# Half of a depthwise convolution on TensorE, with merged weights, while VectorE makes the other half

## The chip, the cores and the metric

One NeuronCore of a Trainium2 chip runs the whole program. It has five engines with instruction streams of their own: TensorE (PE), VectorE (DVE), ScalarE (ACT), GpSimd (POOL) and SyncE (SP), which issues the DMAs here. The metric is the time of one execution on the device in microseconds; of several executions the median is given.

## The reference, cut to what matters

The input `x` is [4, 64, 64, 96]: four images. Two state-space layers (L0, L1) are followed by two layers of attention and feed-forward. Each state-space layer first normalises over groups of three channels and then does this (E = 192 inner channels):

```python
xz = jnp.einsum('bhwc,ec->bhwe', x, in_proj_w)
xx, z = jnp.split(xz, 2, axis=-1)
xc = conv_general_dilated(xx in NCHW, conv_w, (1, 1), [(1, 1), (1, 1)], feature_group_count=E) + conv_b
xc = silu(xc)
# four directions k of the image: row-wise, column-wise, and both reversed
x_dbl = einsum('bkdl,kcd->bkcl', xs, x_proj_weight)   # step sizes, B and C
delta = softplus(einsum('bkrl,kdr->bkdl', dts, dt_projs_weight) + bias)
h = exp(delta * A) * h + delta * B * u                # scan over 4096 positions
y = sum over directions of (C . h) + u * D; layer norm; y * silu(z); out_proj
```

The convolution is depthwise, 3 by 3, with a border of zeros: each of the 192 channels is a sum of nine shifted copies of its own plane, each times one number. The projection before it is linear and acts on channels alone. So projection and convolution together can also be written as nine matrices of 96 by 96, one for each tap: the matrix of tap t is the projection's weight times the tap's weight of each output channel.

## The kernel before, in words

**Stages.** The images are worked on in two pairs for each of the two state-space layers: four phases. `Scans.run` does for each phase first `prepare` (with `finish` of the phase before woven into it), then `scan_phase`. After the fourth scan comes its `finish` alone, then `token_layers`. All four scans have an order written out by hand. Everything else is emitted by Python generators, and a scheduler then decides the order in which each engine's instructions stand; that order is fixed when the program runs, and an engine never passes an instruction that waits. The order spoken of below is that of the built program.

**Preparation.** `prepare` takes the statistics of both images (`bn_stats`, L192), and then handles image 0 and image 1 of the pair. `convolve` does one image. Its 192 channels are two halves h of 96 (96 partitions each). For each half it loads the image in eight pieces of 512 positions (`rawi`, L252, two buffers), projects each on TensorE (L258), writes the result on ScalarE into a padded plane `xp` of 66 by 66 (L261), and then makes eight chunks of 512 outputs: ScalarE does tap 0 (L275), VectorE adds the other eight taps one instruction each (L277), ScalarE applies SiLU (L280). After a half's convolution it copies the result in another layout to `xu` (two buffers, L285) and stores it with eight DMAs to `ud` (L291), for the `D` term in `finish`. All of this is float32. `xp` and the rest of `convolve` live in a pool "conv" with one buffer, and image 1's pool can take the memory only when image 0's last `ud` store has landed.

`steps` makes, for one image, one chunk and one axis, the projections L300 (both halves are contracted, so both must be done) and L317, softplus, `du` and the three-part bfloat16 `delta`, and stores them. There are 32 such steps in a phase: 16 of image 0, into which image 1's `convolve` is woven (two `next(other)` a step), then 16 of image 1.

**Pace of finish.** Each `yield` of `prepare` adds `ph.beside` to an account; each whole unit in it lets `finish` go on by one `yield`. `finish` takes the phase's scan output in four quarters: permutation matmuls L603 and additions L612 for two halves, ScalarE copies L619, layer norm on VectorE (L642 to L657), gate L669 and L672, transposes L683, output projection L694. The first phase has no `finish` beside it.

Of the kernel before, what the change touches and what calls it, by code (L numbers as in the profile page):

```python
# [70 lines left out]
def view(t, off, *dims):  # L71

    return bass.AP(t.tensor, t.offset + off, [t.ap[0]] + [list(d) for d in dims])
# [57 lines left out]
class Scans:  # L131
# [19 lines left out]
    def prepare(self, ph):  # L151

        nc, cst, a, pre = self.nc, self.cst, self.a, ph.pre
        ph.gs = self.keep.tile([C, 2, 2], F32, name="gs", bufs=3)
        ph.delta = [
            self.dram.tile([G, NP16, E, TC], BF16, name="delta", bufs=2 * NC) for _ in range(NC)
        ]


        ph.du = [  # L160
            self.dram.tile([2, G, E + PITCH, TC], F32, name="du", bufs=2 * NC) for _ in range(NC)
        ]
        ph.bc = [self.dram.tile([NS // 2, G, 4, TC], F32, name="bc", bufs=2 * NC) for _ in range(NC)]
        ph.ud = self.dram.tile([C, 2, HW, 2, 64], F32, name="ud")
        ph.y = self.dram.tile([64, G, 2, 2, NEB, 16 * EB], F32, name="y")
        x = ph.x_in[ph.pair]

        with self.tc.tile_pool(name="prep", bufs=1) as wp, self.tc.tile_pool(
            name="steps", bufs=2
        ) as sp:  # L170

            def load(name, shape, at=0):
                t = wp.tile([at + shape[0]] + shape[1:], F32, name=name)
                nc.sync.dma_start(t[at:], a[pre + name])
                return t

            xp = load("x_proj", [C, 2, 2, XD2])
            dt_w = load("dt_w", [XD2 - 2 * NS, 2, E], at=2 * NS)
            conv_b = load("conv_b", [C, 2])
            ds = load("Ds", [C, 2, K])  # L180
            dsum = wp.tile([C, 2], F32, name="dsum")
            nc.vector.tensor_reduce(dsum, ds, mybir.AxisListType.X, ALU.add)
            yield


            st = wp.tile([C, 2, 8, 6], F32, name="st")
            with self.tc.tile_pool(name="stats", bufs=2) as rp:
                for hl in range(8):
                    raw = rp.tile([C, 8, 2, 64], F32, name="raw")
                    nc.sync.dma_start(raw, x[:, hl * 8 : hl * 8 + 8])  # L190
                    for i in range(2):
                        nc.vector.bn_stats(st[:, i, hl], raw[:, :, i])  # L192
                    yield
            for i in range(2):
                mv = wp.tile([C, 2], F32, name="mv")
                nc.vector.bn_aggr(mv, st[:, i].rearrange("p c s -> p (c s)"))
                ps = self.bank()
                nc.tensor.matmul(ps[:C, :1], cst.group, mv[:, 0:1], start=True, stop=True)
                gs = ph.gs[:, i]
                nc.vector.tensor_copy(gs[:, 0:1], ps[:C, :1])  # L200
                d = wp.tile([C, 1], F32, name="d")
                nc.vector.tensor_tensor(d, mv[:, 0:1], gs[:, 0:1], ALU.subtract)
                nc.vector.scalar_tensor_tensor(d, d, d, mv[:, 1:2], ALU.mult, ALU.add)
                ps = self.bank()
                nc.tensor.matmul(ps[:C, :1], cst.group, d, start=True, stop=True)
                ln = wp.tile([C, 2], F32, name="ln")
                neg_rsqrt(nc, cst, ps[:C, :1], ln[:, 0:1], gs[:, 1:2], ln[:, 1:2])
                nc.vector.tensor_scalar_mul(gs[:, 1:2], gs[:, 1:2], -1.0)
                yield
            in_w = wp.tile([C, E], F32, name="in_w")  # L210
            nc.sync.dma_start(in_w, a[pre + "in_proj_w"][:, :E])
            taps = load("conv_w", [C, 2, 9])

            xc = [wp.tile([C, 2, L], F32, name="xc", bufs=2) for _ in range(2)]
            ph.beside = 1.0
            yield
            yield from self.convolve(ph, 0, x, xc[0], in_w, taps, conv_b, dsum)
            ph.beside = 0.6
            other = self.convolve(ph, 1, x, xc[1], in_w, taps, conv_b, dsum)
            for i in range(2):  # L220
                for c in range(NC):
                    for k in range(2):
                        yield from self.steps(ph, sp, xc[i], xp, dt_w, i, k, c)
                        for _ in range(2):
                            next(other, None)
                            yield
                for _ in other:
                    yield
                ph.beside = 1.25

    def convolve(self, ph, i, x, xc, in_w, taps, conv_b, dsum):


        nc = self.nc
        with self.tc.tile_pool(name="conv", bufs=1) as cp:
            gs = ph.gs[:, i]
            scaled = cp.tile([C, E], F32, name="in_ws")
            nc.vector.tensor_scalar_mul(scaled, in_w, gs[:, 1:2])
            shift = cp.tile([C, 2], F32, name="shift")
            for h in range(2):  # L240
                ps = self.bank()
                nc.tensor.matmul(
                    ps[:C, :1], scaled[:, h * C : (h + 1) * C], gs[:, 0:1], start=True, stop=True
                )
                nc.vector.tensor_scalar_mul(shift[:, h : h + 1], ps[:C, :1], -1.0)
            for h in range(2):
                xp = cp.tile([C, PAD, PAD], F32, name="xp")
                for edge in (xp[:, 0, :], xp[:, PAD - 1, :], xp[:, 1 : PAD - 1, 0], xp[:, 1 : PAD - 1, PAD - 1]):
                    nc.vector.memset(edge, 0.0)
                for hl in range(8):  # L250
                    raw = cp.tile([C, TC], F32, name="rawi", bufs=2)
                    nc.sync.dma_start(  # L252
                        raw.rearrange("c (a p) -> c a p", p=64), x[:, hl * 8 : hl * 8 + 8, i]
                    )
                    if hl % 2 == 0:
                        yield
                    ps = self.bank()
                    nc.tensor.matmul(  # L258
                        ps[:C], scaled[:, h * C : (h + 1) * C], raw, start=True, stop=True
                    )  # L260
                    nc.scalar.activation(  # L261
                        view(xp, (1 + hl) * PAD + 1, (1, 8), (8 * PAD, 8), (8, 8)),
                        ps[:C].rearrange("c (a h w) -> c a h w", a=8, h=8),
                        AF.Identity,
                        bias=shift[:, h : h + 1],
                    )
                for c in range(NC):
                    yield
                    acc = xc[:, h, c * TC : (c + 1) * TC]
                    for tap in range(9):  # L270
                        dy, dx = divmod(tap, 3)
                        src = xp[:, ROWS * c + dy : ROWS * (c + 1) + dy, dx : dx + HW]
                        w = taps[:, h, tap : tap + 1]
                        if tap == 0:
                            nc.scalar.activation(rows(acc), src, AF.Copy, scale=w)  # L275
                        else:
                            nc.vector.scalar_tensor_tensor(  # L277
                                rows(acc), src, w, rows(acc), ALU.mult, ALU.add
                            )
                    nc.scalar.activation(acc, acc, AF.Silu, bias=conv_b[:, h : h + 1])  # L280
                for hl in range(8):
                    if hl % 2 == 0:
                        yield
                    xu = cp.tile([C, 8, 64], F32, name="xu", bufs=2)
                    nc.scalar.activation(  # L285
                        xu.rearrange("c w (a b) -> c w a b", b=8),
                        view(xc[:, h], hl * HW, (1, 8), (8 * HW, 8), (8, 8)),
                        AF.Copy,
                        scale=dsum[:, h : h + 1],
                    )  # L290
                    nc.sync.dma_start(ph.ud[:, h, 8 * hl : 8 * hl + 8, i], xu)  # L291
# [647 lines left out]
def laid_out(i):  # L939
    x = i["x"].reshape(NP, 2, 8, 8, 8, 8, C)  # L940
    a = {"x": x.transpose(0, 6, 3, 5, 1, 2, 4).reshape(NP, C, HW, 2, 64)}
    for n, gamma, beta in (("L0_", "ln_gamma", "ln_beta"), ("L1_", "out_norm_g", "out_norm_b")):
        p = n + "conv_"
        a[n + "in_proj_w"] = i[p + "in_proj_w"].T
        a[n + "conv_w"] = i[p + "conv_w"].reshape(2, C, 9).transpose(1, 0, 2)
        a[n + "conv_b"] = i[p + "conv_b"].reshape(2, C).T
        a[n + "Ds"] = i[p + "Ds"].reshape(K, 2, C).transpose(2, 1, 0)
        a[n + "gamma"] = i[p + gamma][None]
# [49 lines left out]
```

## Time and profile before

| | us |
|---|---|
| median of 3 runs | 11881.9 (11853.94 to 11897.37) |
| the profiled execution, whole | 11923.01 |
| its span, first to last instruction | 11921.2 |
| first scan instruction of the four phases (L435) at | 723.3, 3441.2, 6149.6, 8860.7 |
| last scan instruction of the four phases starts at about | 2593, 5301, 8009, 10717 |
| image 1's `convolve` begins (L238, second time in the phase) at | 189.1, 2808.3, 5518.9, 8225.6 |

The four stretches between scans are what the change touches: 723 us at the front and some 850 us before each of the other three scans. A row of a timeline gives start, length, engine, line, operation, tiles, shape and count, and in brackets how long the engine stood idle before it and what ended that. A float32 matmul shows as two records, one for each of its two passes. Groups give the least, median and largest length of one record in nanoseconds.

### The profile page before, as it was taken

Reading aid. Unit: us, or ns where it says so; the run is one execution under the profiler, and the core shown is the slowest. Engines: PE = TensorE matmul, PEld = TensorE weight load, DVE = VectorE, ACT = ScalarE, POOL = GpSimd, SP = SyncE. Lnnn points to the kernel's source line nnn. Section 1 sums busy time; section 2 is a strip of 40 time slices with the busy share of each in tenths; the row PEclk is TensorE's granted clock in tenths of the full one; section 3 lists DMA queues with packets and bytes.
Section 4 is the critical chain, followed back from the end, with each engine's and each line's share of the span. In section 5 each row is a group of like instructions: output and inputs, shape, how many; then the busy total and the mean of one; then the engine's idle time right before and its main releaser. Section 6 shows DMA issues by size and latency. Waiting matters only on the chain.

```text
span 11921.2 us, 337611 instructions
## 1 busy us (share of the span) xinstructions
PE 8549.8 (72%) x144992; PEld 4586.7 (38%) x144992; DVE 9991.8 (84%) x10247; ACT 7335.1 (62%) x12106; POOL 7480.2 (63%) x2316
## 2 busy tenths in 40 slices
PE   4557777765767777765767777766667777777777
PEld 1124444432334444442334444433234444444333
DVE  6679999977779999987769999986769999993667
ACT  4556666655556666655556666655557666662556
POOL 0169999961159999970149999980149999980000
PEclk8578999986679999986679999887578898998887
DMA  3677777765677777765777777765677777763110
GB/s 99 192 244 250 253 255 254 251 208 144 201 241 256 253 253 251 253 217 146 204 229 258 256 253 251 253 217 149 198 226 255 255 255 253 253 229 124 18 22 11
DMA packets 952266, 2501.22 MB, mean 210 GB/s; under 512 B 324494, under 2 KB 607220, under 8 KB 819316
## 3 DMA queue, kind: packets, MB, share of 16 engines
q1 hardware_dynamic: 950772, 2479.63, 63.0%
q8 instruction: 1142, 18.71, 0.7%
q14 instruction: 352, 2.88, 0.1%
HBM read 1965.42 MB, written 513.80 MB: 208 GB/s over the span
## 4 chain that ended last, share of the span: by engine, by line
DMA 57%; PE 12%; DVE 11%; SPq 10%; ACT 5%; issue 3%; POOL 2%; POOLq 0%; DVEq 0%; ACTq 0%
DMA h<-du 53%; SPq L408 9%; DVE xc L277 4%; PE f L603 2%; POOL parts L331 2%; PE d L317 1%; DVE dl L328 1%; PE f L683 1%; PE c L300 1%; DVE du_sb L327 1%; PE f L694 1%; DVE parts L332 1%; DMA yk<-y 1%; PE f L669 1%; PE f L612 1%
## 5 line engine op out<-in xcount | busy, mean ns | idle before, releaser
L418 POOL TENSOR_TENSOR h<-h,b 128x1536 f32<-128x1536 f32 x2048 | 7020.9, 3461 | 574.0 <-DMA h<-du 229.6
L435 DVE TENSOR_TENSOR_SCAN h<-a,carry,h 128x512 f32<-128x512 f32 x5376 | 6353.3, 1259 | 202.8 <-POOL h L418 199.4
L428 ACT ACTIVATE a<-a,a_col 128x512 f32<-128x512 f32 x6144 | 4038.5, 664 | 1888.6 <-PE a L424 1852.8
L453 PEld LDWEIGHTS y<-h,cw 128*32 128x32 f32 x131072 | 2785.0, 128 | 3534.2 <-issue 1369.4
L453 PE MATMUL y<-h,cw 128*32 128x48 f32 x131072 | 3658.4, 266 | 522.4 <-DVE h L435 205.3
L424 PE MATMUL a<-dlt,rep 72*128 72x512 bf16 x6144 | 2534.2, 422 | 1352.5 <-DVE h L435 1254.1
L331 POOL CAST parts<-dl 96x1024 bf16<-96x1024 f32 x256 | 431.2, 1688 | 2687.6 <-DVE dl L328 1979.4
L465 ACT COPY d<-y 128x384 f32<-128x384 f32 x2048 | 979.7, 478 | 467.7 <-PE y L453 414.9
L435 DVE TENSOR_TENSOR_SCAN h<-a,h 128x512 f32<-128x512 f32 x768 | 868.2, 1200 | 179.7 <-ACT a L428 113.4
L277 DVE SCALAR_TENSOR_TENSOR xc<-xp,conv_w,xc 96x512 f32<-96x512 f32 x1024 | 716.3, 760 | 154.2 <-ACT xc L275 110.0
L424 PEld LDWEIGHTS <-rep 72*128 72x128 bf16 x6144 | 487.5, 98 | 849.3 <-issue 613.9
L317 PE MATMUL d<-xd,dt_w 7*96 7x512 f32 x1024 | 532.0, 885 | 263.6 <-ACT dl L325 141.2
L835 POOL MEMSET tn<- 1x4096 f32 x8 | 27.8, 3506 | 861.5 <-PE pa L855 515.4
L300 PE MATMUL c<-xc,x_proj 96*103 96x512 f32 x512 | 442.0, 1002 | 115.7 <-ACT xp L261 54.6
L327 DVE TENSOR_TENSOR du_sb<-dl,xc 96x1024 f32<-96x1024 f32 x256 | 409.9, 1607 | 123.6 <-ACT dl L325 67.2
L603 PE MATMUL f<-yk,perm 128*128 128x384 f32 x1024 | 415.6, 549 | 106.4 <-DMA yk<-y 81.0
L325 ACT ACTIVATE dl<-d 96x1024 f32<-96x1024 f32 x256 | 257.7, 1018 | 348.6 <-DVE parts L332 259.2
L328 DVE TENSOR_TENSOR dl<-dl,parts 96x1024 f32<-96x1024 f32 x256 | 309.8, 1216 | 190.7 <-ACT parts L326 187.8
L332 DVE TENSOR_TENSOR parts<-dl,parts 96x1024 bf16<-96x1024 f32 x256 | 326.2, 1280 | 170.0 <-POOL parts L331 168.8
L317 PEld LDWEIGHTS d<-xd,dt_w 7*96 7x96 f32 x1024 | 160.0, 216 | 586.5 <-ACT xd L303 200.1
L258 PE MATMUL c<-rawi,in_ws 96*96 96x512 f32 x256 | 195.5, 874 | 241.3 <-ACT xp L261 101.6
L370 ACT ACTIVATE cw<-c,gmask 128x256 f32<-128x256 f32 x512 | 285.5, 569 | 129.3 <-DMA dlt<-delta 66.7
(119 smaller groups left out, 5764.0 us busy)
## 6 DMA issues: line engine op xcount, KB each, us to landing
h<-du SPq DMA_DIRECT2D x1024, 768.0 KB
h<-du SPq DMA_DIRECT2D x2048, 384.0 KB
du<-du_sb SPq DMA_DIRECT2D x512, 384.0 KB
delta<-parts SPq DMA_DIRECT2D x256, 576.0 KB
dlt<-delta SPq DMA_DIRECT2D x512, 288.0 KB
y<-d SPq DMA_DIRECT2D x2048, 48.0 KB
yk<-y SPq DMA_DIRECT2D x256, 384.0 KB
ud<-xu SPq DMA_DIRECT2D x128, 192.0 KB
```

The costliest lines, as they stand in the source:

```text
L277: nc.vector.scalar_tensor_tensor(rows(acc), src, w, rows(acc), ALU.mult, ALU.add)
L300: nc.tensor.matmul(rows(ps[:XD2]), xp[:, k, h], u[:, h], start=h == 0, stop=h == 1)
L317: nc.tensor.matmul(ps[:, m], dt_w[part, k, m * C : (m + 1) * C], xd[part], start=True, stop=True)
L331: nc.gpsimd.tensor_copy(parts[:, 1], delta)
L408: self.nc.sync.dma_start(u.h[32 * first : 32 * (first + quarters), e : e + n].rearrange("p e t -> p (e t)"), source.rearrange("a g e t -> ...
L418: self.nc.gpsimd.tensor_tensor(h, h, b, ALU.mult)
L424: self.nc.tensor.matmul(u.a[n], self.cst.rep[:, h], u.dl[:, e], start=True, stop=True)
L428: self.nc.scalar.activation(u.a[n], u.a[n], AF.Exp, scale=u.ph.a_col[:, at : at + 1])
L435: self.nc.vector.tensor_tensor_scan(u.h[:, n], u.a.pop(n), u.h[:, n], 0.0 if u.c == 0 else u.ph.carry[:, at : at + 1], ALU.mult, ALU.add,)
L453: self.nc.tensor.matmul(view(u.y[32 * j : 32 * j + 32], l2 * EB, (8 * EB, 4), (1, EB)), u.ph.cw[u.c][:, l1, 8 * j + l2], view(u.h, 64 * l1 ...
L465: self.nc.scalar.copy(u.d[:, :, :, l1], u.y[:, : 32 * EB].rearrange("p (t h x) -> p t h x", t=4, h=2))
L603: nc.tensor.matmul(ps[:, : 4 * C].rearrange("p (w v e) -> p w v e", w=4, v=nv), cst.perm[:, k], view(t, off, (sw if k < 2 else -sw, 4), (1 ...
```

## The change

For image 0 of each pair `convolve` gets a scratch plane `xn`, which lies in the memory of image 1's result. It goes through the loop over h once, with h = 1. While h = 1 is projected and padded as before, VectorE also writes the normalised input of the image into `xn` (L271 of the new file: subtract the mean, multiply by the reciprocal deviation; no projection). Then, for each of the eight chunks, TensorE makes half 0 with nine accumulating matmuls of `merged` weights on shifted windows of `xn`, and ScalarE applies SiLU from PSUM. VectorE makes half 1 with its eight taps as before. The merged weights come from one DMA that broadcasts the taps to 96 partitions (96 x 864) and one multiplication by the projection's weight. The stores to `ud` of both halves stand together after the convolution. `ph.beside` in this part is 1.6 where it was 1.0, since the part has 20 yields where it had 32. Image 1 is convolved as before.

```diff
-            ph.beside = 1.0
+            ph.beside = 1.6
             yield
-            yield from self.convolve(ph, 0, x, xc[0], in_w, taps, conv_b, dsum)
+            xn = xc[1].rearrange("c h l -> c (h l)")[:, : PAD * PAD].rearrange("c (a b) -> c a b", b=PAD)
+            yield from self.convolve(ph, 0, x, xc[0], in_w, taps, conv_b, dsum, xn)
...
-    def convolve(self, ph, i, x, xc, in_w, taps, conv_b, dsum):
+    def convolve(self, ph, i, x, xc, in_w, taps, conv_b, dsum, xn=None):
...
-            scaled = cp.tile([C, E], F32, name="in_ws")
-            nc.vector.tensor_scalar_mul(scaled, in_w, gs[:, 1:2])
+            first = 0 if xn is None else 1
+            scaled = cp.tile([C, 2 - first, C], F32, name="in_ws")
+            nc.vector.tensor_scalar_mul(
+                scaled.rearrange("c h e -> c (h e)"), in_w[:, first * C :], gs[:, 1:2]
+            )
+            if xn is not None:
+                merged = cp.tile([C, 9, C], F32, name="merged")
+                nc.sync.dma_start(
+                    merged, self.a[ph.pre + "conv_t"].unsqueeze(0).broadcast_to([C, 9, C])
+                )
+                nc.vector.tensor_tensor(
+                    merged, merged, in_w[:, :C].unsqueeze(1).broadcast_to([C, 9, C]), ALU.mult
+                )
             shift = cp.tile([C, 2], F32, name="shift")
-            for h in range(2):
+            for h in range(first, 2):
...
-            for h in range(2):
+            for h in range(first, 2):
                 xp = cp.tile([C, PAD, PAD], F32, name="xp")
...
+                    if xn is not None:
+                        nc.vector.tensor_scalar(
+                            view(xn, (1 + hl) * PAD + 1, (1, 8), (8 * PAD, 8), (8, 8)),
+                            raw.rearrange("c (a h w) -> c a h w", a=8, h=8),
+                            gs[:, 0:1],
+                            gs[:, 1:2],
+                            ALU.subtract,
+                            ALU.mult,
+                        )
...
+                    if xn is not None:
+                        ps = self.bank()
+                        for tap in range(9):
+                            dy, dx = divmod(tap, 3)
+                            nc.tensor.matmul(
+                                rows(ps[:C]),
+                                merged[:, tap],
+                                xn[:, ROWS * c + dy : ROWS * (c + 1) + dy, dx : dx + HW],
+                                start=tap == 0,
+                                stop=tap == 8,
+                            )
+                        nc.scalar.activation(
+                            xc[:, 0, c * TC : (c + 1) * TC], ps[:C], AF.Silu, bias=conv_b[:, 0:1]
+                        )
...
-                for hl in range(8):
+                for h, hl in [(h, hl) for h in (range(2) if first else (h,)) for hl in range(8)]:
                     if hl % 2 == 0:
                         yield
```

More of the change, by code (lines that the diff above doesn't have):

```diff
@@ L236, in convolve @@
             gs = ph.gs[:, i]
-            scaled = cp.tile([C, E], F32, name="in_ws")
-            nc.vector.tensor_scalar_mul(scaled, in_w, gs[:, 1:2])
+            first = 0 if xn is None else 1
[11 more added lines that the diff above has]
+                )
             shift = cp.tile([C, 2], F32, name="shift")
-            for h in range(2):
+            for h in range(first, 2):
                 ps = self.bank()
                 nc.tensor.matmul(
-                    ps[:C, :1], scaled[:, h * C : (h + 1) * C], gs[:, 0:1], start=True, stop=True
+                    ps[:C, :1], scaled[:, h - first], gs[:, 0:1], start=True, stop=True
                 )
                 nc.vector.tensor_scalar_mul(shift[:, h : h + 1], ps[:C, :1], -1.0)
-            for h in range(2):
+            for h in range(first, 2):
                 xp = cp.tile([C, PAD, PAD], F32, name="xp")
-                for edge in (xp[:, 0, :], xp[:, PAD - 1, :], xp[:, 1 : PAD - 1, 0], xp[:, 1 : PAD - 1, PAD - 1]):
-                    nc.vector.memset(edge, 0.0)
+                for t in (xp,) if xn is None else (xp, xn):
+                    for edge in (t[:, 0, :], t[:, PAD - 1, :], t[:, 1 : PAD - 1, 0], t[:, 1 : PAD - 1, PAD - 1]):
+                        nc.vector.memset(edge, 0.0)
                 for hl in range(8):
@@ L256, in convolve @@
                         yield
+                    if xn is not None:
[7 more added lines that the diff above has]
+                        )
                     ps = self.bank()
                     nc.tensor.matmul(
-                        ps[:C], scaled[:, h * C : (h + 1) * C], raw, start=True, stop=True
+                        ps[:C], scaled[:, h - first], raw, start=True, stop=True
                     )
@@ L945, in laid_out @@
         a[n + "conv_w"] = i[p + "conv_w"].reshape(2, C, 9).transpose(1, 0, 2)
+        a[n + "conv_t"] = i[p + "conv_w"].reshape(E, 9)[:C].T
         a[n + "conv_b"] = i[p + "conv_b"].reshape(2, C).T
```

## The prediction

> **What bounds the kernel now.** I read the page first, then the busy times by stretches of 50 and 25 us, then the timelines of DVE, PE and ACT in the first preparation (0 to 250 us) and the second (2590 to 3080 us), and last the built order of both programs.
>
> ```profile
> span 11921.2 us, 337611 instructions
> ...
> DMA 57%; PE 12%; DVE 11%; SPq 10%; ACT 5%; issue 3%; POOL 2%; POOLq 0%; DVEq 0%; ACTq 0%
> ...
> L277 DVE SCALAR_TENSOR_TENSOR xc<-xp,conv_w,xc 96x512 f32<-96x512 f32 x1024 | 716.3, 760 | 154.2 <-ACT xc L275 110.0
> ```
>
> The chain is mostly the scans (h<-du), which the change leaves alone. Its L277 instructions, 716 us in all, lie in the preparations, so only these can change. What sets their length? In the first, DVE shows it:
>
> ```profile
> 58.23 43.03 DVE L277 SCALAR_TENSOR_TENSOR xc<-xp,conv_w,xc 96x512 f32<-96x512 f32 x64 [18.11 <-ACT xc L275]
> ...
> 126.07 39.93 DVE L277 SCALAR_TENSOR_TENSOR xc<-xp,conv_w,xc 96x512 f32<-96x512 f32 x60 [1.88 <-ACT xp L261]
> ...
> 189.09 0.32 DVE L238 TENSOR_SCALAR in_ws<-in_w,gs 96x192 f32<-96x192 f32 x1 [12.71 <-DMA ud<-xu]
> ```
>
> Half 0 takes DVE 43 us (0.67 us a tap), half 1 another 43; between them lies the refill of the padded plane (101 to 123 us), behind them the last copies and stores. Image 1 begins when the last store to ud has landed, at 189.1; the second of the 32 steps stands behind image 1's first projections on PE. So 189.1 is the milestone: what comes after it keeps its work. In the second preparation the same two blocks stand at 2664.8 and 2739.3, with finish beside them:
>
> ```profile
> 2664.80 41.47 DVE L277 SCALAR_TENSOR_TENSOR xc<-xp,conv_w,xc 96x512 f32<-96x512 f32 x62 [10.85 <-ACT xc L275]
> ...
> 2739.26 40.78 DVE L277 SCALAR_TENSOR_TENSOR xc<-xp,conv_w,xc 96x512 f32<-96x512 f32 x61
> ...
> 2808.28 0.32 DVE L238 TENSOR_SCALAR in_ws<-in_w,gs 96x192 f32<-96x192 f32 x1 [2.89 <-DMA du<-du_sb]
> ```
>
> The stretches say whether PE has room there (columns: PE, PEld, DVE, ACT, POOL busy with counts, granted clock, DMA share, GB/s):
>
> ```profile
> 2675.00:2700.00 25.00, 16.90 (x76) 11.34 (x74) 25.00 (x39) 7.38 (x13) 0.00 (x0) 0.84 0.67 189
> 2700.00:2725.00 25.00, 6.67 (x7) 1.59 (x8) 17.90 (x55) 16.45 (x18) 0.00 (x0) 0.50 0.27 57
> 2725.00:2750.00 25.00, 14.97 (x50) 7.78 (x48) 21.62 (x39) 18.03 (x24) 0.00 (x0) 0.77 0.22 48
> 2750.00:2775.00 25.00, 4.85 (x9) 1.63 (x8) 25.00 (x39) 11.23 (x13) 0.00 (x0) 0.50 0.01 5
> ```
>
> Between the two blocks PE is mostly idle and DVE is full.
>
> **The price of a tap on PE.** The nearest row is L258, the same shape (96x512 float32 from 96 partitions, two passes):
>
> ```profile
> L258 PE MATMUL c<-rawi,in_ws x36: 1057/1061/1167, 39.8 to 194.9; 96*96 96x512 f32 x36
> ```
> ```profile
> L258 PE MATMUL c<-rawi,in_ws x16: 590/593/595, 2652.7 to 2688.5; 96*96 96x512 f32 x16
> ```
> ```profile
> 2687.22 1.88 PE L258 MATMUL c<-rawi,in_ws 96*96 96x512 f32 x4
> 2688.94 2.96 PE L669 MATMUL f<-in_w,xm 96*128 96x192 f32 x16
> ```
>
> The first is of 0 to 200 us, the second of 2650 to 2700. At full clock two matmuls take 2688.94 - 2687.22 = 1.72 us, 0.86 each; at half clock 1.70 each (40.75 to 41.60 is one pass). The granted clock reads 1.00 before 200 us although the passes are slow, so I go by the durations. Which price holds? The Trainium skill, "TensorE: Matmul & The Clock Gate", on the HAM clock gate: some 3.4 us of sustained work release the full clock, a like idle time takes it back. Its section on "psum-queue depth-cycling" speaks against this change: a PE that changes PSUM banks and idles briefly between groups goes up and down. The taps change banks after every nine matmuls, with two buffers. The row decides for full clock: from 2650 on, permutations, additions and projections change banks every four or five matmuls and still run at 590 ns. The bank itself is free in time: a group of nine takes 9 x 0.86 = 7.7 us, the SiLU that frees it 0.72 (row of L280). So 72 x 0.86 = 61.9 us, and some 3 us of warming up where PE was cold; by the other rule 72 x 1.70 = 122.4. L300 for the column axis reads a strided window at the same least 591 ns, so the windows of xn cost nothing extra; weight loads already hide at full clock (L603 changes weights with each matmul: 8 records in 2680.27 to 2682.88, the same 1.7 ns a column).
>
> **First preparation, step by step.** Removed: half 0's 64 taps on DVE, 8 projections on PE, 8 L261 and 8 L275 on ACT, 8 loads of rawi. Added: a load of 96x864 float32 (332 KB) in front of the rawi loads, and the next phase's same load between the statistics' loads. The latter (393 KB each) come every 2.5 us, so each costs about 2 us: +4, both taken as exposed. The multiplication (864 columns; L656 takes 1.76 us for 1536, so 1.0), the eight xn writes (L661, 0.54 us, up to 1.26 when it waits) and xn's border (0.43) lie on DVE, which idles 18 us before its first tap: nothing. Without that cover it would be 6 us.
> - PE's taps begin behind the last projection, 58.99 + 3.79 = 62.8, plus 4: 66.8. In the built order all 72 stand before the first L300.
> - They end at 66.8 + 61.9 + 3 = 131.7, SiLU at 132.4. DVE's half 1 (43 us) ends near 105 and hides under this.
> - Now 16 copies with stores, in place of 8. On SP they stand in one queue with bc, du and delta, so a late du would hold them, and image 1's loads stand behind. Price: the first 8 took 102.9 to 119.0 (2.0 each), the last 8, with du and delta between them, 170.4 to 189.1 (2.3 each). 16 x 2.15 = 34.4.
> - Image 1 begins at 166.8 instead of 189.1: **22.3 us earlier**.
>
> **The other three.** The next phase's merged load stands at the end of the preparation before, under the scan: nothing.
> - Taps begin at 2665.5. In PE's order, finish's second half-quarter stands between them: 16 L603 at 0.65 and 16 L612 at 0.21 make 13.8 us. PE ends at 2665.5 + 61.9 + 13.8 = 2741.2, SiLU at 2742.
> - DVE does 46 taps and then the layer norm's statistics, which now wait until PE is through three groups (about 2697); the second set waits for the sixth group (2726). Behind these waits stand 18 taps and the rest of that layer norm: its first slice ends near 2758, and du behind it at about 2763, before 2781. No loss against PE's end.
> - 16 copies with stores, 34.4. ACT also does 4 L672, 4 L690, two each of L303/304, L325, L326 and two table loads: 4 x 0.49 + 4 x 0.58 + 2 x 0.68 + 4 x 1.0 + 2 x 1.28 = 12.2 us. Most fits in the gaps of the copies (2.15 less 1.2 each); I charge 5. Image 1 begins at 2781.4 instead of 2808.3: 26.9 earlier.
> - But finish is behind. Before, the gate, transposes and output projection of its second slice lay in the wait for the stores (2790 to 2808). Now they follow image 1's start: 8 L669 at 0.40, 16 L683 at 0.27, 4 L694 at 0.86 are 11 us of PE. In the built order PE has caught up by the twelfth step of 32, and the last third is the same as before. Before, steps 8 to 12 left PE idle for 40 of 75 us (2925 to 3000). Bounds: nothing, if all of it falls there; 17, if the chain of 2790 to 2808 is paid again. I take 6, nearer to that slack. Left: **21 us in each of three**.
>
> Sum: 22.3 + 3 x 21 = 85 us. Scans, last finish and token layers keep order and work. The profiled execution took 11923.0 (span 11921.2 and 1.8 around it), 0.35% over the median; 85 off it gives 11838, and off the median 11881.9 - 85 = **11797 us**.
>
> **Rivals.**
> - *The lag is paid in full.* Layer norm, gate and copies of finish wait on each other, and steps of image 1 queue behind them; then 10 to 15 more are lost in each of three preparations, and 22 + 3 x 8 = 46 is left: 11836; with half the first one's gain lost too, 11847. For it: DVE and PE both idle in turn after 2808 (DVE 10 us at 2853), a chain and no full engine. Against it: before the eighth step finish does less than it did, 7 us of PE where it was 16.
> - *The change does nothing*, because DMA sets the end of a preparation whatever precedes. For it: at 500 to 650 us DMA is busy 0.82 to 0.84. Against it: from 200 to 500 it is 0.5 to 0.66, so nothing is piled up when the second half of the steps begins. 11882.
> - *PE stays at half clock* (the other side). 72 x 0.84 = 60 us more in each of four: image 1 begins 38 us later than before in the first, and about 39 in the others: 11882 + 155 = 12037. It decides from 0.29 us more a tap (21 / 72), when a third of the passes are slow. For it: PE ran all of 0 to 200 us so. Against it: it idled before each of those pairs, and now nothing stands between the groups.
> - *More is won*: copies at 1.5 us each on a quiet queue, lag free: 30 us each, 11762.
>
> **How the numbers follow.** Forecast 0.60, its own range 11770 to 11825; lag in full 0.16, 11825 to 11860; nothing 0.06; half clock or another stall of its size 0.12; more 0.06. Time: 11797. The range that holds 8 in 10 goes from 11765 to 11880: it leaves out the half clock and pieces of the ends. About 0.5% (59 us, 11822) is what a measurement can tell from no change. Faster: the forecast but for its edge, and more, 0.65. Same: 0.22. Slower: half clock and 0.01 beyond, 0.13.
>
> **What would show it.** Right: tap passes of 590 ns with 0.43 between starts; image 1's in_ws near 167, 2781 and alike in the rest; 65 to 75 us from the first to the last tap; L277 down to 768 instructions. Wrong: passes over 1000 ns within the taps (half clock); image 1 early but the scan of the second phase not 40 us earlier than 3441 (lag, or DMA); copies xu at over 2.6 us each (then the doubled stores took the gain).

## The result and the profile after

The changed kernel takes 11802.2 us (median of five runs, 11786.4 to 11833.0), the kernel before 11881.9 in the same session. The ratio is 0.9932, with the interval 0.9915 to 0.9948: 62 to 101 us less. The forecast was 11797.

The page of the changed kernel, in three of its lines (span; chain of work that ended last; the group of taps that VectorE still makes):

```profile
span 11800.4 us, 338304 instructions
...
DMA 58%; PE 14%; SPq 10%; DVE 8%; ACT 5%; issue 3%; POOL 2%; DVEq 0%; POOLq 0%; ACTq 0%
...
L313 DVE SCALAR_TENSOR_TENSOR xc<-xp,conv_w,xc 96x512 f32<-96x512 f32 x768 | 540.3, 760 | 88.8 <-ACT xc L311 72.7
```

VectorE's taps went from 1024 to 768 instructions and from 716 to 540 us busy. In the chain, VectorE's share fell from 11% to 8% and TensorE's rose from 12% to 14%. That is a trade inside the preparations; the shares do not say what it was worth. Two timelines do. TensorE's in the first preparation (start, length, engine, line, operation):

```profile
54.93 3.88 PE L280 MATMUL c<-rawi,in_ws 96*96 96x512 f32 x4 [1.01 <-DMA rawi<-in_x]
58.60 63.41 PE L295 MATMUL c<-xc,merged 96*96 96x512 f32 x144
121.85 1.88 PE L336 MATMUL c<-xc,x_proj 96*103 96x512 f32 x4
...
163.39 3.70 PE L280 MATMUL c<-rawi,in_ws 96*96 96x512 f32 x4 [1.82 <-DMA rawi<-in_x]
```

VectorE's in the first and second preparation:

```profile
61.00 41.40 DVE L313 SCALAR_TENSOR_TENSOR xc<-xp,conv_w,xc 96x512 f32<-96x512 f32 x62 [0.52 <-ACT xc L311]
...
160.40 0.32 DVE L240 TENSOR_SCALAR in_ws<-in_w,gs 96x192 f32<-96x192 f32 x1 [20.07 <-DMA ud<-xu]
...
2748.97 0.32 DVE L240 TENSOR_SCALAR in_ws<-in_w,gs 96x192 f32<-96x192 f32 x1 [12.02 <-DMA ud<-xu]
```

All 144 passes (72 float32 matmuls) run in one stretch of 63.4 us from 58.6. VectorE's half, under them, is done at 102.4, some 20 us before TensorE's. Image 1 begins (L240, the prediction's milestone) at 160.4 in place of 189.1. The last run of copies before it starts 47.6 us earlier (122.8 in place of 170.4) and takes 18.9 us longer (37.6 for 16 in place of 18.7 for 8): that is the 28.7. The clock question is answered by the groups of the two stretches (least, median, largest length in ns). First preparation:

```profile
L295 PE MATMUL c<-xc,merged x144: 590/592/1061, 58.6 to 121.4; 96*96 96x512 f32 x144
```

Second preparation:

```profile
L295 PE MATMUL c<-xc,merged x144: 590/592/595, 2629.1 to 2705.7; 96*96 96x512 f32 x144
```

Both ran at full clock, but for the first four passes of the cold one (1061 ns three times, then 761).

Cut into stages (each preparation from the end of the scan before, or from 0, to the first scan instruction; all from the traces):

| us | before | after | gain |
|---|---|---|---|
| preparation 1 | 723.3 | 693.7 | 29.6 |
| preparation 2 | 847.2 | 825.0 | 22.2 |
| preparation 3 | 847.0 | 824.6 | 22.4 |
| preparation 4 | 850.8 | 825.7 | 25.1 |
| image 1 begins, after the preparation's start | 189.1, 214.3, 216.4, 215.7 | 160.4, 191.3, 190.3, 192.1 | 28.7, 23.0, 26.1, 23.6 |
| four scans, summed | 7449.8 | 7431.5 | 18.3 |
| last finish and token layers | 1203.1 | 1199.9 | 3.2 |

The preparations gained 99.3 us, where 85 were predicted. The two spans differ by 120.8, of which 18.3 lie in the scans, which the change does not touch. Those are not counted as a gain: over the 13 traces of this case the four scans sum to anything between 7401 (e4) and 7467 (e9). With the second traces of the two kernels (e1 and e10 below) in place of one or both, the preparations' gain is 92 to 107 us.

### The profile page after: what moved, and what is told of

It reads as the page before. It is cut to its first block, busy times and chain, and to the rows that moved or that the text cites. A ratio compares the mean times of both kernels' runs of the same rounds, so it can differ in the third digit from the quotient of the medians.

```text
span 11800.4 us, 338304 instructions
## 1 busy us (share of the span) xinstructions
PE 8705.9 (74%) x145496; PEld 4653.3 (39%) x145496; DVE 9854.5 (84%) x10023; ACT 7289.4 (62%) x12052; POOL 7461.4 (63%) x2316
## 3 DMA queue, kind: packets, MB, share of 16 engines
q1 hardware_dynamic: 926132, 2474.66, 63.4%
## 4 chain that ended last, share of the span: by engine, by line
DMA 58%; PE 14%; SPq 10%; DVE 8%; ACT 5%; issue 3%; POOL 2%; DVEq 0%; POOLq 0%; ACTq 0%
DMA h<-du 53%; SPq L444 9%; PE f L639 3%; DVE xc L313 2%; PE c L295 2%; POOL parts L367 1%; PE d L353 1%; DVE parts L368 1%; DVE dl L364 1%; DVE du_sb L363 1%; DMA yk<-y 1%; PE f L719 1%; PE c L336 1%; PE f L648 1%; PE f L730 1%
## 5 line engine op out<-in xcount | busy, mean ns | idle before, releaser
L313 DVE SCALAR_TENSOR_TENSOR xc<-xp,conv_w,xc 96x512 f32<-96x512 f32 x768 | 540.3, 760 | 88.8 <-ACT xc L311 72.7
L353 PEld LDWEIGHTS d<-xd,dt_w 7*96 7x96 f32 x1024 | 162.3, 220 | 621.0 <-ACT xd L339 231.0
L362 ACT CAST parts<-dl 96x1024 bf16<-96x1024 f32 x256 | 265.2, 1041 | 145.1 <-DMA delta<-parts 143.6
```

The lines of the kernel that those rows point to most:

```text
L313: nc.vector.scalar_tensor_tensor(rows(acc), src, w, rows(acc), ALU.mult, ALU.add)
L353: nc.tensor.matmul(ps[:, m], dt_w[part, k, m * C : (m + 1) * C], xd[part], start=True, stop=True)
```

## The experiments

The theory to be tested: TensorE's 62 us of taps and the copies behind them lie on the path in full, VectorE's half lies beside them, and an earlier start of image 1 shortens the preparation one for one. The rivals: it is VectorE's relief that counts, tap for tap (256 less to do); finish, pushed behind image 1's start, takes part of the gain back (the prediction charged 6 us for it, with 0 and 17 as bounds); or the doubled block of stores does. Diffs are against the changed kernel.

**The kernel before, once more (e1).** Nothing is edited.

> The kernel before, unchanged, for a second trace: how far do its own stages repeat? Every theory expects the four preparations again at 723, 847, 847 and 851 us, to within 5 us; the scans may differ by more.

Measured: 11883.2 us; preparations 720.5, 843.9, 844.3, 852.6, in sum 3261.4 (3268.3 in the trace shown above); image 1 begins at 189.0, 214.0, 215.8, 217.5. Scans 1851.7, 1850.9, 1862.3, 1850.1, where the first trace has 1870.7, 1861.3, 1860.4, 1857.4. So preparations repeat to some 3 us each, single scans only to 20, and a few microseconds must be read from the preparations and not from the whole.

**TensorE's taps twice (e2).** The nine matmuls of each group run twice. The first of the second nine starts the sum anew, so the result is the same and only TensorE's time is added.

```diff
-                        for tap in range(9):
+                        for tap in [*range(9), *range(9)]:
```

> TensorE makes each chunk of half 0 twice over (18 matmuls; the second nine start the bank anew, so the result is the same). If TensorE's taps lie on the path that leads to image 1's start: 72 x 0.86 = 62 us more in each of four preparations, image 1 begins 62 later in each, about 12,050 us in all. If VectorE's half or the stores set it: clearly less, under 20 us each.

Measured: 12055.0 us. The timelines of TensorE and VectorE in the first preparation:

```profile
59.26 125.04 PE L295 MATMUL c<-xc,merged 96*96 96x512 f32 x288
```

```profile
222.71 0.32 DVE L240 TENSOR_SCALAR in_ws<-in_w,gs 96x192 f32<-96x192 f32 x1 [19.90 <-DMA ud<-xu]
```

61.6 us more of matmuls put image 1's start 62.3 us later and made the preparations 59.3, 59.9, 61.4 and 62.2 us longer. What is added to TensorE's taps is paid in full; nothing of it hides. The run does not show that all 62 us would be won if the taps were taken away: VectorE's half ends only 20 us before TensorE's and would then set the pace.

**Some of the taps back on VectorE (e3).** In each preparation 24 of the removed 64 taps come back to VectorE as work on a scratch tile that nobody reads (0.67 us each, 16 us).

```diff
+            if first:
+                spare = cp.tile([C, TC], F32, name="xu", bufs=2)
+                nc.vector.memset(spare, 0.0)
...
+                            if first and tap < 4:
+                                nc.vector.scalar_tensor_tensor(
+                                    rows(spare), src, w, rows(spare), ALU.mult, ALU.add
+                                )
```

> VectorE does 24 of its 64 taps a second time in each preparation, into a scratch tile that nobody reads (16 us). If VectorE's half is covered by TensorE's: the first preparation keeps its length to 3 us (VectorE ends near 118, TensorE near 121), the three others, where layer norm stands behind the taps on VectorE, gain 0 to 16; about +15 us on the changed kernel in all, 11,815. If the gain was VectorE's lighter load: 16 us more in each of four, +64, 11,866.

Measured: 11771.7 us, ratio to before 0.9906 (0.9889 to 0.9923); preparations 691.7, 828.6, 828.9, 823.5, in sum 3.7 us over those of the changed kernel, where 4 x 16 = 64 us of VectorE work were added. The timelines of VectorE (its last taps) and TensorE in the first preparation:

```profile
113.69 3.87 DVE L316 SCALAR_TENSOR_TENSOR xc<-xp,conv_w,xc 96x512 f32<-96x512 f32 x5
157.82 0.32 DVE L240 TENSOR_SCALAR in_ws<-in_w,gs 96x192 f32<-96x192 f32 x1 [17.43 <-DMA ud<-xu]
```

```profile
58.96 63.42 PE L298 MATMUL c<-xc,merged 96*96 96x512 f32 x144
```

VectorE now ends at 117.6, still before TensorE's 122.4, and its added work is covered. So the relief did not count tap for tap: 24 of the 64 taps could come back for almost nothing. More than 24 were not tried. That the median lies below the changed kernel's is no effect of the edit on the preparations; the scans of this trace sum to 7410.8, those of the changed kernel's to 7431.5.

**Half 1's stores first (e4, and e11 on the third chip).** VectorE's half is ready some 20 us before TensorE's, yet its copies and stores stand behind those of half 0.

```diff
-                for h, hl in [(h, hl) for h in (range(2) if first else (h,)) for hl in range(8)]:
+                for h, hl in [(h, hl) for h in ((1, 0) if first else (h,)) for hl in range(8)]:
```

> The copies and stores of half 1 (VectorE's, done some 15 us before TensorE's half) come before those of half 0. If the last store's landing, which releases image 1, sets the rest: image 1 begins 12 to 14 us earlier in each of four, 45 to 55 us off the changed kernel, about 11,750. If DMA or finish sets the length of the preparations: image 1 begins earlier and the preparations stay as long as in the changed kernel, 11,800.

Measured: 11752.1 us, ratio to before 0.9888 (0.9872 to 0.9905). Preparations 676.8, 813.4, 817.0, 816.6: 45 us less than the changed kernel's. The busy times by stretches show why (columns: stretch, length, then PE, PEld, DVE, ACT, POOL busy with counts, granted clock, DMA share, GB/s). The changed kernel:

```profile
105.00:125.00 20.00, 18.73 (x44) 6.85 (x42) 0.00 (x0) 4.28 (x6) 0.00 (x0) 1.00 0.00 1
125.00:145.00 20.00, 4.43 (x8) 1.46 (x8) 7.16 (x6) 15.89 (x16) 3.00 (x2) 0.53 0.65 158
145.00:165.00 20.00, 2.41 (x6) 1.39 (x7) 1.00 (x7) 7.18 (x6) 0.00 (x0) 0.50 0.68 163
```

With half 1 first:

```profile
105.00:125.00 20.00, 18.44 (x43) 6.68 (x41) 0.00 (x0) 11.47 (x12) 0.00 (x0) 1.00 0.37 80
```

In the changed kernel the DMA engines do nothing (1 GB/s) while TensorE makes its last groups, and then 16 stores come at once. In e4 all eight copies of half 1 and their stores go under TensorE's groups (ScalarE is 11.5 us busy in place of 4.3 in this stretch; eight copies are left after the taps, not 16), and image 1's L240 runs at 142.9, 17.5 us earlier. The timelines of VectorE and TensorE with half 1 first:

```profile
142.91 0.32 DVE L240 TENSOR_SCALAR in_ws<-in_w,gs 96x192 f32<-96x192 f32 x1 [2.89 <-DMA ud<-xu]
```

```profile
151.87 3.70 PE L280 MATMUL c<-rawi,in_ws 96*96 96x512 f32 x4 [7.78 <-DMA rawi<-in_x]
```

The first projection of image 1 (L280) comes only 11.5 us earlier (163.4 in the changed kernel), since it waits for its load; e5 shows why that matters.

> Half 1's stores first, again, with more rounds. Preparations of 677, 813, 817 and 817 us to within 5, so 40 to 50 us under the changed kernel: 0.988 to 0.990 of before.

e11 is the same kernel on another chip, next to the changed one (e10): 11774.4 us, ratio to before 0.9887 (0.9873 to 0.9902); preparations 681.1, 820.0, 817.1, 812.5, in sum 31 us under e10's, and the medians of the two (11774.4 and 11825.6) are 51 apart. This is the version that beats both kernels.

**Four tiles for the copies (e5).** The copies go in turn through `xu` and `rawi`, whose two buffers are idle then, so that ScalarE waits less for a store to free one.

```diff
-                    xu = cp.tile([C, 8, 64], F32, name="xu", bufs=2)
+                    xu = cp.tile([C, 8, 64], F32, name="rawi" if first and hl % 4 > 1 else "xu", bufs=2)
```

> Image 0's copies use four tiles in turn (xu and the rawi tiles, free by then) in place of two; order of the halves as in the changed kernel. If the copies wait for their stores to land (2.3 us a copy and store, of which the copy is 1.2): 16 x 0.5 to 0.9 = 8 to 14 us off each preparation, 11,750 to 11,770. If the queue that issues the stores with du and delta is the limit: under 3 us each.

Measured: 11824.0 us, ratio to before 0.9952 (0.9937 to 0.9968). L240 of image 1 comes 10.4, 12.2, 8.9 and 8.8 us earlier than in the changed kernel, and the preparations are the same: 3170.7 in sum against 3169.0. This broke the theory's last clause: the start of image 1 (L240) need not set the length. SP's own queue shows what does. The changed kernel:

```profile
155.52 2.35 SPq L327 DMA_DIRECT2D ud<-xu  x2
160.24 7.19 SPq L265 DMA_DIRECT2D rawi<-in_x  x4
```

The four tiles:

```profile
146.03 1.40 SPq L327 DMA_DIRECT2D ud<-rawi  x2
147.50 1.48 SPq L348 DMA_DIRECT2D bc<-xd  x2
149.10 0.88 SPq L366 DMA_DIRECT2D du<-du_sb  x2
150.07 0.79 SPq L369 DMA_DIRECT2D delta<-parts  x1
150.91 4.06 SPq L366 DMA_DIRECT2D du<-du_sb  x2
155.06 1.22 SPq L369 DMA_DIRECT2D delta<-parts  x1
156.38 10.73 SPq L265 DMA_DIRECT2D rawi<-in_x  x4
```

With two tiles the first step's `bc`, `du` and `delta` went out between the stores. With four, all 16 stores went first, those eight DMAs after them, and image 1's `rawi` loads stand behind on the same queue: issued from 156.4 on, where L240 had run at 150.0. They also take longer to land, 6.7 us from issue to the first projection where the changed kernel needs 3.2, in a stretch in which the DMA share is 0.77 in place of 0.68. TensorE's timeline with four tiles:

```profile
163.06 3.70 PE L280 MATMUL c<-rawi,in_ws 96*96 96x512 f32 x4 [11.88 <-DMA rawi<-in_x]
```

That is 163.1 against 163.4: image 1's first projection, and not L240, is the gate. The stage times agree in the main. Over the ten traces other than e7 to e9 (where finish comes in, see below) the stretch from image 1's first projection to the first scan instruction varies less than that from L240 in each of the four preparations:

| us, least to largest | from the first projection | from L240 |
|---|---|---|
| preparation 1 | 524.9 to 531.1 | 530.3 to 540.8 |
| preparation 2 | 622.3 to 632.0 | 629.9 to 652.2 |
| preparation 3 | 621.0 to 637.3 | 628.5 to 656.9 |
| preparation 4 | 625.4 to 628.7 | 631.7 to 648.0 |

One value speaks against it: e4's first preparation has 524.9 from the projection and 533.8, the usual length, from L240; its repeat e11 has 530.5 and 539.8. For e4 this means: of the 12.7 to 17.5 us that L240 won, 6.9 to 11.5 reached the first projection, and the last three preparations won 11.6, 7.6 and 9.2.

**Both edits of e4 and e5 (e6).**

> Half 1's stores first and four tiles together. Half 1's eight copies then lie wholly under TensorE's last groups, and the eight behind cost 1.2 to 1.6 us each: image 1 begins 5 to 8 us earlier than with half 1's stores first alone, some 20 us off that in all, 11,730. If the queue is the limit: the same as half 1's stores first alone, 11,752.

Measured: 11772.9 us, ratio to before 0.9914 (0.9894 to 0.9935); preparations 679.7, 819.9, 826.6, 818.7. Not the 11,730 of the first expectation: no better than e4. L240 stands at 142.3, 167.7, 169.8, 170.7, in the last three 7 to 8 us earlier than in e4, but the first projections of image 1 are where they were: 151.6, 188.1, 189.4, 191.3 against 151.9, 187.6, 189.7, 188.6. The same gate. That the preparations are 3.0, 6.5, 9.6 and 2.1 us longer than e4's, on another chip, is not explained by it; a single preparation repeats to within 6.6 us (e4 and e11).

**Finish slower and faster beside image 0 (e7, e8).** The account `ph.beside` in front of image 1; in e7 the steps after it make up for it.

```diff
-            ph.beside = 1.6
+            ph.beside = 1.0
...
-                ph.beside = 1.25
+                ph.beside = 1.38
```

```diff
-            ph.beside = 1.6
+            ph.beside = 2.4
```

> The pace of finish beside image 0's convolution is 1.0 as it was, and 1.38 in place of 1.25 in the last part, so that it still ends. If finish's lag is nearly free (as in the changed kernel): image 1 begins 5 to 10 us earlier in the last three, their lengths stay within 5 us of 825. If the lag is paid in full: 10 to 17 us longer each.

> The pace of finish beside image 0's convolution is 2.4 in place of 1.6. If the lag cost some 6 us in each of the last three (the prediction's value): those come back less what TensorE does more before image 1, lengths 818 to 828. If finish in front of image 1 costs more than behind it: 830 to 845.

Measured: 11804.4 us (e7) and 11871.9 (e8). VectorE's timelines at the start of image 1 in the second preparation, e7:

```profile
2728.94 0.32 DVE L240 TENSOR_SCALAR in_ws<-in_w,gs 96x192 f32<-96x192 f32 x1 [6.93 <-DMA ud<-xu]
```

and e8:

```profile
2765.90 0.32 DVE L240 TENSOR_SCALAR in_ws<-in_w,gs 96x192 f32<-96x192 f32 x1 [13.47 <-DMA x<-xo]
```

In e8 image 1 begins only when a store of finish's output (`x<-xo`) has landed; its first projection comes 16.7, 17.3 and 14.9 us later than in the changed kernel, and the preparations are 16.2, 19.7 and 17.0 longer. In e7 L240 comes 5.6, 4.9 and 5.4 us earlier and the first projection 7.3, 6.2 and 7.5, and the preparations are 3.5, 3.6 and 0.2 longer, not shorter. In these two runs, one execution each, more of finish in front of image 1 is paid in full, and more of it behind image 1 wins nothing: there the lag of finish takes back the whole of the earlier start. (e7 also changes the pace of the last part, and does not separate the two.)

**No copies for image 0 (e9).** The copies and stores for the term with D are left out for image 0, so that term is missing there; two large stores from `xp` into the same place stand in for the writes to `ud`.

```diff
+                    if xn is not None and c < 2:
+                        nc.sync.dma_start(ph.ud[:, c, :, i], xp[:, 1 : PAD - 1, 1 : PAD - 1])
...
+                    if first:
+                        continue
```

> Image 0's sixteen copies and stores to ud are left out; in their place two stores write other data of the same size while TensorE makes its taps, so the term with D is not computed for image 0. Nothing then stands between the end of the convolution and image 1's first loads. If the landing of those loads sets the rest: it comes near 128 instead of 163 in the first preparation, and all four are some 30 to 35 us shorter than the changed kernel's 694, 825, 825 and 826; about 11,670. If the steps' own stores or finish set it from there on: under 20 us each.

Measured: 11741.9 us (on that chip the changed kernel took 11825.6, the kernel before 11908.7). The timelines of VectorE and TensorE in the first preparation:

```profile
121.09 0.32 DVE L240 TENSOR_SCALAR in_ws<-in_w,gs 96x192 f32<-96x192 f32 x1 [18.21 <-PE c L297]
```

```profile
126.13 2.38 PE L280 MATMUL c<-rawi,in_ws 96*96 96x512 f32 x4
```

L240 now waits for TensorE's taps themselves, and the first projection comes 37.3 us earlier than in the changed kernel (163.4). In the first preparation 35.2 us of that are won: the copies are on the path almost in full. In the others the first projection comes 35.9, 36.3 and 37.3 earlier, but only 16.7, 19.6 and 26.8 are won, in two of them less than the 20 at which the expectation turned to another limit. There something else takes over when image 1 starts that early. Finish, which the first preparation does not have, is the likely one; no run separates it out.

**The changed kernel again (e10).** Nothing is edited.

> The changed kernel, unchanged, beside the version with half 1's stores first on the same chip. Preparations of 694, 825, 825 and 826 us to within 5; 0.9915 to 0.9948 of before.

Measured on the third chip, beside e9 and e11: 11825.6 us, ratio to before 0.9922 (0.9905 to 0.9939); preparations 688.9, 822.2, 822.7, 827.8, in sum 3161.6 (3169.0 in the first trace). The result repeats; the first preparation was 4.8 us shorter.

## Why the prediction was right

- **Clock.** 0.86 us a matmul was the price to take. 36 tap passes in a row of the second preparation take 15.6 us, 0.43 each. The rule on "psum-queue depth-cycling" (the Trainium skill, "TensorE: Matmul & The Clock Gate"), which spoke for a clock that goes down and up between groups, did not bite: in the second preparation the groups of nine stayed at 590 to 595 ns. Its condition hardly arose, since TensorE idled for at most 1.2 us from the first tap to the last there, and not at all in the first preparation. In the first, 63.4 - 61.9 = 1.5 us were lost to warming up, where 3 were charged. The rival of half clock (12037) is out.
- **Start of the taps in the first preparation: wrong by 8 us.** Predicted 66.8, measured 58.6. The 58.99 + 3.79 from which it came was not the end of half 0's projections; that row already belonged to half 1, and half 0's were through at 57.9. And the merged loads, charged 4 us, cost 0.9 (58.8).
- **Copies: wrong by 3 us the other way.** 16 x 2.15 = 34.4 predicted, 37.6 measured (122.8 to 160.4), 2.35 each. In the second preparation it is 42.7 from the last tap's end, with 39.4 predicted. A copy often waits 0.6 to 2.1 us for a store to free its tile.
- **First preparation, sum.** -8.2 (start) - 1.5 (warm-up) + 3.3 (copies) = -6.4: image 1 at 160.4 and not 166.8. Gain 29.6, predicted 22.3.
- **The others.** The taps began 71.4 us into the second preparation and ended at 148.6; predicted were 71.5 and 147.2, so finish's work between the groups, charged at 13.8 us, was sized well (15.3). Its first `du` stood at 169.1, predicted 169, 22 us before image 1 began. With the dearer copies the milestone won 23.0, 26.1 and 23.6, where 26.9 was predicted.
- **Finish's lag.** 6 us were charged, 0.8, 3.7 and -1.5 are found (milestone's gain less the preparation's). The lag was charged 5 us too much on average, and the milestone came 2.7 us less early than forecast: the two errors run in opposite directions, and by this luck 21 each came out near (22.2, 22.4, 25.1). The rival of the lag paid in full (11836) fell with it for the pace of 1.6; moved further behind in e7, finish was paid in full.
- **The milestone itself.** Image 1's start as the thing that sets the length was not quite right: the gate is the landing of image 1's first loads behind it on SP's queue (e5, e6). In the change itself both move together, so no number suffered.
- **The whole.** 99.3 us in the preparations against 85 predicted, and a median only 79.7 lower. That the forecast lies 5 us from the result is thus in part luck: the steps were mis-sized by up to 8 us, and their sum by 14. The interval (62 to 101) holds 99 just so, and with the second traces the preparations' gain lies between 92 and 107; the traces leave open whether the scans give some of it back, since their own spread is larger than what is in question. Of the other rivals, "the change does nothing" is out, with every preparation 22 to 30 us shorter; "more is won" (11762) asked for copies at 1.5 us each, and they took 2.35.

## What to carry to other kernels

Work moved from one engine to another is worth what it shortens on the path, not what the first engine is spared: here VectorE was spared 176 us of taps, of which 24 taps in each preparation could come back for almost nothing. The gain came from making the two halves side by side, with TensorE's 62 us and the 16 stores behind them now the path. When two halves become ready at different times, send the early one out first: with the order of the stores turned round, the idle DMA engines carried half of them under the last matmuls, for another 31 to 45 us. And image 1 began here when its first load landed, which depended on what had been put ahead of it on SP's queue; freeing its memory 9 to 12 us earlier (e5) gained nothing, since the load then stood behind other DMAs.

## What the runs showed of the hardware

- The granted clock reads 1.00 in the first 200 us of the kernel before although its passes there take 1057 ns at the least and 1061 in the median, and 590 at full clock; in that stretch only the lengths tell the clock.
- A strided window of the padded plane costs nothing as a moving operand: 592 ns a pass in the median, where the contiguous projections of the kernel before take 593.
- Scans, where the chain that ended last runs over the loads of `du` (DMA h<-du, 53% of the whole span), differ by up to 20 us each between two runs of the same kernel, and by 66 us in the sum of four over the traces here; the preparations of one kernel repeat to within 6.6 each and to 7 or 8 in their sum.
